# A list-scheduled attention and MLP block: products of originals in streams of their own, traced DMA constants, and new leads and places for every stage

## The chip, the cores and the metric

The kernel runs on one core of one Trainium2 chip. The metric is device time in microseconds (us) of one execution, and the median over the runs is what counts. The engines named below are TensorE (PE, matmuls and transposes), VectorE (DVE), ScalarE (ACT), GpSimd (POOL) and SyncE (SP), which here only issues DMAs.

## The reference, cut to what matters

One transformer block with cross attention, all in fp32: B = 8 batches of 256 tokens `x` with 512 features, a context of the same shape, 16 heads of 32 features, an MLP of 2048.

```python
x = layer_norm(hidden_states, ln1_w, ln1_b)
q = (x @ q_w + q_b)                     # heads of 32
k = (encoder_hidden_states @ k_w + k_b)
v = (encoder_hidden_states @ v_w + v_b)
scores = einsum('bhqd,bhkd->bhqk', q, k) * scale
scores = where(mask, scores, finfo.min)
out = einsum('bhqk,bhkd->bhqd', softmax(scores), v)
hidden = out @ cproj_w + cproj_b + residual
y = layer_norm(hidden, ln2_w, ln2_b)
y = gelu(y @ fc_w + fc_b, approximate=True) @ proj_w + proj_b
return hidden + y
```

## The kernel before

**Tiling and stages.** The batches are worked in two groups of four (`g` = 0, 1). For each group the context tiles (`ct`) and x tiles (`xt`, after a layer norm whose results are `xn`) are transposed on TensorE into `ps_c` and `ps_x` banks and copied to SBUF; then come the k, q and v projections; the attention core in 32 units per group (four heads of one batch: scores `s`, softmax `pr`, transposes of the probabilities `ps_pt`, copied to `pt`, and values `av`, scaled by reciprocals `r` into `att`); the output projection `o` with the residual `hid`; the second layer norm and its transposes `ps_y`; and the MLP products `fc` and `pr`. k, q and v are stored to DRAM (`kd`, `qd`, `vd`) and loaded again unit by unit (`ku`, `qu`, `vu`); reciprocals take the same way (`rd`, `r`).

**Seven products instead of eight.** Every large product is cut into 2x2 blocks and computed by Winograd's scheme in `quad`: seven block products P1 to P7, in the order 1, 2, 6, 7, 5, 3, 4, into three PSUM banks X, Y and W. P1 and P2 take blocks of both operands as they are (originals). P3 to P7 take a sum of blocks on at least one side: `kws`, `qws`, `vws` of the weights, `c0t` and `x0t` of the tokens, computed on VectorE or GpSimd (`plus`). P6, P5 and P3 add onto P1 in bank X. The MLP uses the scheme on two levels (`grown2`, `grown`); the sums of its weights, `fw` and `pw`, are computed during the attention core and stored to DRAM (`fcd`, `prd`); those of its inputs are `y1t`, `z1t` and `z1i` for group 1.

**What sets the order.** No loop issues instructions directly. Every operation is recorded in an `Order` with the engines that could run it and a cost on each. `times` gives each TensorE operation a due time `vt`, spread evenly over the window of its stream (`WINDOWS`, one stream per stage and group); every other operation is due ahead of its earliest user, by its own cost, for DMAs also `DMA_FIXED + 1.0 + mb / DMA_RATE`, and by its `lead`. `run` then simulates the engines, and each takes among the ready operations the one due first, under limits:

```python
if o.vt - (t - lag) > AHEAD[e]:
    continue
...
soon = bisect.bisect_left(vts.get("C", []), last + BORROW)
lent = sorted(s[0] for s in free_slots["C"])[soon:]
```

`AHEAD` is how far ahead of its due time an operation may be placed on an engine; the other two lines let `quad` borrow PSUM banks of the C kind (5, for transposes, scores and values) beside its own three, less those that a C user due within `BORROW` will want. SBUF tiles come from a pool of slots: one slot of 128x1024 holds, one after another, tiles of many names, so a row in the profile or the order shows the name that first held it (`ct` in a row may hold x tiles, `kw_222<-in_x_dram` is an x tile). The engine of each operation, and its place, are thus decided when the program is built; on the chip each engine runs its list in order.

**DMAs.** All loads and stores are issued by SP, in the order of its list, over eight semaphore lanes: a DMA is not issued before the one eight places earlier has landed. `load` and `store` record them.

**Lines the change touches.** Constants at lines 30 to 34, `times` (100), `run` with `room` (135, 177), `INPUTS` and `WINDOWS` (365 to 376), `load` (461), `mask_of` (548: a mask row is loaded into `mu` and turned into a bias `mb` on VectorE or GpSimd; the `mu` tile of batch b + 4 is that of batch b), `quad` (658) and its callers `project_turned`, `project_plain`, `keys_of`, `values_of`, and `attention_inputs` (1074), which records the loads, transposes and projections of a group.

## Time and profile before

| | |
|---|---|
| median of 3 runs | 753.72 us (751.98 to 754.6) |
| the profiled execution | 753.82 us |
| its span | 752.0 us |
| mean granted TensorE clock | 0.993 |
| DMA | 144.06 MB, mean 192 GB/s |
| ACT, largest idle group | `pr` activations, 108.0 us idle, 104.2 of it behind VectorE's `st` |

The median of the three runs is the time before. The profile is of one execution of its own, and "span" is the time from its first to its last recorded instruction. In a row of a timeline stand start, duration, engine, line, operation, tiles with shapes and, in brackets, the idle time of that engine just ahead and what ended it. In a row of a table by stretches stand, after the stretch, its length, then for PE, PEld (weight loads), DVE, ACT and POOL the busy time with the count of instructions, then the granted clock, the busy share of the DMA engines and GB/s. In a row of a group stand line, engine, operation, tiles and count, then busy time, mean ns of one, and the idle time ahead.

### The profile page before, as it was taken

What the parts mean: (1) busy time and instruction counts of PE and PEld (TensorE: products, weight loads), DVE (VectorE), ACT (ScalarE), POOL (GpSimd) and SP (SyncE); (2) the same over time, 40 slices, a digit from 0 to 9 for tenths busy, and PEclk for the clock granted to TensorE, in tenths of its full rate; (3) what the DMA queues carried; (4) which work ended last, traced back from release to release, by engine and by line L of the source; (5) the groups of instructions that cost most, each with busy time, mean ns of one, the idle gap of its engine ahead of it and who ended that gap; (6) DMA issues with size and microseconds to landing.
All of it is one profiled execution on the core that took longest, in us unless ns stands there. A gap on an engine that the chain in (4) does not pass through costs nothing.

```text
span 752.0 us, 13728 instructions
## 1 busy us (share of the span) xinstructions
PE 710.5 (94%) x4753; PEld 563.5 (75%) x4753; DVE 596.0 (79%) x1356; ACT 293.9 (39%) x829; POOL 331.4 (44%) x290
## 2 busy tenths in 40 slices
PE   6799999989999799899999999989999999899997
PEld 4345675457655577678787779989998888799997
DVE  4895788668796688788788887997688877989784
ACT  3300665448365383664556893120001034430000
POOL 2631075464640331410101388556873126859650
PEclk9999999999999899999999999999999999999999
DMA  7818889788568845355444451365767455463641
GB/s 253 293 58 311 288 274 316 222 266 283 164 223 290 279 147 188 91 159 165 136 140 145 136 194 57 118 210 173 259 214 220 147 160 169 147 229 115 223 144 57
DMA packets 119332, 144.06 MB, mean 192 GB/s; under 512 B 14136, under 2 KB 82272, under 8 KB 119264
## 3 DMA queue, kind: packets, MB, share of 16 engines
q1 hardware_dynamic: 119264, 143.19, 59.3%
q8 instruction: 38, 0.62, 0.3%
q14 instruction: 30, 0.25, 0.1%
HBM read 98.59 MB, written 44.56 MB: 190 GB/s over the span
## 4 chain that ended last, share of the span: by engine, by line
PE 77%; DVE 11%; DMA 7%; issue 3%; SPq 1%; ACT 1%; POOL 0%; DVEq 0%; POOLq 0%
PE fc_X L506 12%; PE pr_X L506 11%; PE fc_W L506 6%; PE ps_pt L831 6%; PE pr_W L506 5%; PE s L506 4%; PE o_X L506 4%; PE av L506 4%; PE q_X L506 3%; PE fc_Y L506 3%; PE v_X L506 3%; PE k_X L506 3%; PE pr_Y L506 2%; PE o_W L506 2%; PE q_W L506 2%
## 5 line engine op out<-in xcount | busy, mean ns | idle before, releaser
L808 ACT ACTIVATE pr<-pr,st 128x256 f32<-128x256 f32 x256 | 127.4, 501 | 108.0 <-DVE st L802 104.2
L802 DVE CUSTOM_DVE_ANT_0 pr<-s,mb 128x256 f32<-128x256 f32 x256 | 91.6, 419 | 10.6 <-PE s L506 10.4
L831 PEld LDWEIGHTS ps_pt<-ident,pr 128*128 128x128 f32 x512 | 59.7, 142 | 20.8 <-issue 7.2
L991 ACT ACTIVATE h<-h,cols 128x256 f32<-128x256 f32 x128 | 54.1, 499 | 51.1 <-DVE h L497 43.6
L831 PE MATMUL ps_pt<-ident,pr 128*128 128x128 f32 x512 | 71.0, 276 | 2.5 <-DVE att L497 1.5
L497 DVE TENSOR_TENSOR h<-fc_X,h 128x512 f32<-128x512 f32 x80 | 54.7, 687 | 14.2 <-PE fc_X L506 13.6
L477 ACT COPY pt<-ps_pt 128x512 f32<-128x512 f32 x87 | 48.5, 576 | 21.8 <-PE ps_pt L831 21.6
L808 ACT ACTIVATION_READ_ACCUMULATOR pr<-pr,st 128x1 f32 x256 | 48.9, 191 | 0.0
L477 ACT COPY e<-pr_X 128x256 f32<-128x256 f32 x4 | 1.5, 373 | 112.3 <-PE pr_X L506 112.3
L506 PE MATMUL av<-pt,vu 128*32 128x256 f32 x512 | 35.7, 390 | 4.1 <-DVE pt L477 3.9
L506 PE MATMUL s<-ku,qu 32*128 32x256 f32 x512 | 37.8, 400 | 0.0
L497 DVE TENSOR_TENSOR h<-fc_W,h 128x512 f32<-128x512 f32 x48 | 33.0, 688 | 4.4 <-PE fc_W L506 2.7
L506 PEld LDWEIGHTS s<-ku,qu 32*128 32x128 f32 x512 | 24.0, 184 | 14.2 <-issue 9.6
L506 PEld LDWEIGHTS av<-pt,vu 128*32 128x32 f32 x512 | 13.6, 109 | 24.0 <-issue 8.5
L497 DVE TENSOR_TENSOR po<-pr_X,po 128x256 f32<-128x256 f32 x40 | 16.7, 419 | 18.5 <-PE pr_X L506 18.5
L477 DVE COPY pt<-ps_pt 128x512 f32<-128x512 f32 x41 | 27.2, 680 | 3.1 <-PE ps_pt L831 2.8
L555 POOL TENSOR_SCALAR mb<-mu 128x256 f32<-128x256 uint8 x4 | 1.6, 404 | 52.7 <-DMA mu<-in_mask_BxS_bf_dram 52.7
L614 POOL TENSOR_TENSOR rs_y<-rs_y,neg_half 128x2 f32<-128x2 f32 x8 | 6.0, 753 | 34.5 <-DVE rs_y L611 34.5
L802 DVE DVE_READ_ACCUMULATOR2_ANT st<- 128x1 f32 x256 | 21.1, 83 | 0.0
L497 DVE TENSOR_TENSOR att<-av,r 128x256 f32<-128x256 f32 x32 | 13.5, 421 | 8.0 <-PE av L506 5.5
L497 DVE TENSOR_TENSOR h<-fc_Y,h 128x512 f32<-128x512 f32 x24 | 16.5, 686 | 2.2 <-PE fc_Y L506 1.7
L1128 POOL TENSOR_TENSOR hid<-hid,cb 128x1024 f32<-128x1024 f32 x5 | 14.1, 2822 | 8.8 <-DMA hid<-in_x_dram 5.8
(657 smaller groups left out, 1902.7 us busy)
## 6 DMA issues: line engine op xcount, KB each, us to landing
pl<-prd SPq DMA_DIRECT2D x26, 256.0 KB
fw<-in_L_xattn_fc_w_dram SPq DMA_DIRECT2D x16, 256.0 KB
ku<-kd SPq DMA_DIRECT2D x32, 128.0 KB
qu<-qd SPq DMA_DIRECT2D x32, 128.0 KB
vu<-vd SPq DMA_DIRECT2D x32, 128.0 KB
r<-rd SPq DMA_DIRECT2D x32, 128.0 KB
pw<-in_L_xattn_proj_w_dram SPq DMA_DIRECT2D x32, 128.0 KB
hid<-in_x_dram SPq DMA_DIRECT2D x8, 512.0 KB
```

The lines of the kernel that those rows point to most:

```text
L477: (nc.scalar.copy if e == "ACT" else nc.vector.tensor_copy)(to(), of_())
L497: E[e].tensor_tensor(to(), in0(), in1(), op)
L506: nc.tensor.matmul(o(), l(), r(), start=first, stop=True, skip_group_check=True)
L555: lambda e: E[e].tensor_scalar(tile_of(mb), mu.t, -1.0, FLT_MAX, ALU.add, ALU.mult), lock=True)
L614: lambda e, rs=rs: nc.gpsimd.tensor_tensor(tile_of(rs)[:, 2:4], tile_of(rs)[:, 0:2], neg_half[:, 0:2], ALU.pow), lock=True)
L802: nc.vector.tensor_tensor_reduce(at(p_, pk), at(sb[j], i), tile_of(mb), scale=-SCALE, scalar=FLT_MAX, op0=ALU.add, op1=ALU.min, accum_out= ...
L808: nc.scalar.activation(at(p_, pk), at(p_, pk), AF.Exp, bias=tile_of(st)[:, 8 + c : 9 + c], scale=-1.0, accum_out=tile_of(st)[:, 16 + c : 1 ...
L831: nc.tensor.transpose(at(ps, 2 * kc + i, 1, P), at(pr[j // 2], 2 * (j % 2) + i)[:, ts(kc, P)], ident.t)
L991: lambda e, f=f, b=b, c=c: nc.scalar.activation(at(h[f][b], c), at(h[f][b], c), AF.Gelu_apprx_tanh, bias=col(c_fcb + f * 4 + c), scale=1.0 ...
L1128: lambda e, v=v: E[e].tensor_tensor(v(), v(), cb.t[:, None, :].to_broadcast([P, 2, D]), ALU.add), lock=True)
```

## The change

It alters the planner's numbers and one part of its rules, and records some products in other streams. What is computed stays the same.

- *Streams for products of originals.* `quad` has a parameter `early`: P1, P2 and the copies behind them are recorded in that stream. In group 0 k uses `e0`, v `e1` and q `e2`. The k, v and q projections of group 0 are recorded as k0, k1, v0, q0, q1, v1 instead of k0, q0, v0, k1, q1, v1; weights are loaded in the order k, v, q instead of k, q, v.
- *DMA model.* `DMA_FIXED` 1.7 to 3.0, `DMA_RATE` 0.36 to 0.34, the SP cost of a DMA 0.45 to 0.5.
- *Leads.* A table `LEADS` adds to the lead of each load by its name (from 8.6 for `qw`, 7.7 for `pw`, 5.9 for `xt` and 3.8 for `mu` down to -1.0 for `fl` and `ku`); a mask load gets a lead of 12.0 besides.
- *Windows.* Each stream has three times instead of two, one of them for the middle of its TensorE work, and all are new numbers.
- *Limits.* `AHEAD` VectorE 40 to 66.7, ScalarE 40 to 36.8, GpSimd 40 to 25.4, SP 16 to 26.9; `BORROW` 14.0 to 25.6, where at most two C users of the light kind (`ps_` names other than `ps_pt`) count. `SWITCH` is 0.0. The cost of scores is 0.97 instead of 0.86, that of values 0.9.

```diff
-BORROW = 14.0
+BORROW = 25.6
+SWITCH = 0.0
-AHEAD = {"PE": 1000.0, "DVE": 40.0, "ACT": 40.0, "POOL": 40.0, "SP": 16.0}
+AHEAD = {"PE": 1000.0, "DVE": 66.7, "ACT": 36.8, "POOL": 25.4, "SP": 26.9}
-DMA_FIXED, DMA_RATE, DMA_LANES = 1.7, 0.36, 8
+DMA_FIXED, DMA_RATE, DMA_LANES = 3.0, 0.34, 8
...
-            t0, t1 = windows[name]
+            t0, tm, t1 = windows[name]
...
-                o.vt = t0 + (t1 - t0) * at / total
+                f = 2.0 * at / total
+                o.vt = t0 + (tm - t0) * f if f < 1.0 else tm + (t1 - tm) * (f - 1.0)
...
+        light = lambda b: b.kind == "C" and b.name.startswith("ps_") and not b.name.startswith("ps_pt")
+        vts["heavy"] = [b.vt for b in pending.get("C", []) if not light(b)]
...
-                    soon = bisect.bisect_left(vts.get("C", []), last + BORROW)
+                    heavy = bisect.bisect_left(vts["heavy"], last + BORROW)
+                    soon = heavy + min(2, bisect.bisect_left(vts.get("C", []), last + BORROW) - heavy)
...
-    [("k", 0), ("q", 0), ("v", 0), ("k", 1), ("q", 1), ("v", 1)],
+    [("k", 0), ("k", 1), ("v", 0), ("q", 0), ("q", 1), ("v", 1)],
...
-    "core0": (60, 206), "ctx1": (88, 96), "k1": (94, 130), "v1": (124, 160), "x1": (142, 152), "q1": (152, 190),
+    "core0": (68.9, 154.0, 221.0),
+    "e0": (6.3, 7.3, 8.3),
...
+LEADS = {"fl": -1.0, "res": 2.3, "mu": 3.8, "qw": 8.6, "qu": 4.4, "r": 2.3, "pw": 7.7, "ow": 1.8, "kw": 3.9, "fw": 2.8, "pl": 4.1, "vw": 2.0, "ct": 1.3, "ku": -1.0, "hid": -0.8, "xt": 5.9, "vu": 2.3}
...
-            name, [("SP", 0.45)], list(src), [(b, keys)],
-            lambda e: nc.sync.dma_start(to(), of_()), mb=mb, lead=lead,
+            name, [("SP", 0.5)], list(src), [(b, keys)],
+            lambda e: nc.sync.dma_start(to(), of_()), mb=mb, lead=lead + LEADS.get(name.rstrip("0123456789_"), 0.0),
...
-        load(f"mu{b}", mu, None, lambda: mu.t, lambda: mask[b].partition_broadcast(P), 0.03)
+        load(f"mu{b}", mu, None, lambda: mu.t, lambda: mask[b].partition_broadcast(P), 0.03, lead=12.0)
...
+        stream = T.now
+        if early:
+            T.stream(early)
         prod(1, X, True)
         out_of(X, "11", "t1", True)
         prod(2, Y, True)
         out_of(Y, "11", "c11", False)
+        T.stream(stream)
```

What the planner makes of it is seen in the built order. First the head of SP's list, the loads that begin the program; before:

```order
L464 DMA ct_0_216<-in_ctx_dram 128x512 x2
L464 DMA ct_2_219<-in_ctx_dram 128x512 x2
L464 DMA kw_222<-in_L_xattn_k_w_dram 128x2x256
L464 DMA kw_222<-in_x_dram 128x512
L464 DMA xt_1_225<-in_x_dram 128x512 x2
L464 DMA xt_3_228<-in_x_dram 128x512
L464 DMA xt_3_228<-in_ctx_dram 128x512
```

The same list of the change:

```order
L499 DMA vw_216<-in_L_xattn_v_w_dram 128x2x256
L499 DMA vw_216<-in_ctx_dram 128x512
L499 DMA ct_1_219<-in_ctx_dram 128x512 x2
L499 DMA ct_3_222<-in_ctx_dram 128x512
L499 DMA ct_3_222<-in_L_xattn_k_w_dram 128x2x256
L499 DMA kw_225<-in_L_xattn_k_w_dram 128x2x256
L499 DMA kw_225<-in_ctx_dram 128x512
```

A tile of v weights now stands ahead of the context tiles, and the x tiles that stood in places 6 to 9 come behind context and weights.

On TensorE, in the prologue behind the context transposes, before (rows 33 to 40; `k_0_X` on `c0t` and `kws` is a product of sums, `ps_x` a group of x transposes):

```order
L570 MATMUL ps_x_30_371<-ident,xn_x_00_297 128x128 x2
L570 MATMUL ps_x_30_371<-ident,xt_1_225 128x128
L570 MATMUL ps_x_30_371<-ident,xn_x_11_326 128x128
L506 MATMUL q_0_X<-x_00_347,qw_350 128x512 x2
L506 MATMUL k_0_W<-c0t_367,xt_7_344 128x512 x2
L506 MATMUL q_0_Y<-x_10_377,qw_350 128x512 x2
L506 MATMUL k_0_X<-c0t_411,kws_416 128x512 x2
L506 MATMUL k_0_X<-c0t_332,kws_358 128x512 x2
```

There of the change (rows 31 to 42, behind five products of originals):

```order
L541 MATMUL k_0_W<-c0t_324,kws_261 128x512 x2
L541 MATMUL k_1_Y<-c_10_263,kw_239 128x512 x2
L541 MATMUL k_0_X<-c0t_328,vw_216 128x512 x2
L541 MATMUL v_1_X<-vw_216,c_00_246 128x256 x4
L541 MATMUL k_0_X<-c0t_318,kws_261 128x512 x2
L541 MATMUL v_1_Y<-kw_239,c_10_263 128x256 x4
L541 MATMUL k_0_X<-c_11_305,ct_3_222 128x512 x2
L541 MATMUL k_0_W<-c0t_342,ct_7_231 128x512 x2
L541 MATMUL k_1_X<-c0t_328,vw_216 128x512 x2
L541 MATMUL k_1_W<-c0t_324,kws_261 128x512 x2
L541 MATMUL k_1_X<-c0t_318,kws_261 128x512 x2
L605 MATMUL ps_x_00_478<-ident,qws_431 128x128
```

Before, all four x groups of the first tokens and the first q products stand among the k products; now 16 products of k and v stand ahead of the first x transposes, of which six groups follow one another from there.

On SP at the loads of group 1's x tiles (the `in_x_dram` rows; `prd` rows store sums of proj weights, `mu_129` is a mask load), before:

```order
L464 DMA ku_1465<-kd_0_12_131 128x256
L464 DMA qu_1472<-qd_0_12_135 128x256
L470 DMA prd_116<-pw0s_1447 128x4x256
L464 DMA mu_129<-in_mask_BxS_bf_dram 128x256
L470 DMA vd_1_11_150<-kws_358 128x512
L464 DMA ct_7_246<-in_x_dram 128x512
L464 DMA kws_416<-in_x_dram 128x512
L464 DMA xt_7_344<-in_x_dram 128x512
```

The same place of the change:

```order
L499 DMA vu_1517<-vd_0_22_141 128x2x128
L499 DMA kw_239<-in_x_dram 128x512
L499 DMA vw_216<-in_x_dram 128x512
L499 DMA kws_261<-in_x_dram 128x512
L499 DMA xt_3_1557<-in_x_dram 128x512
L505 DMA vd_1_11_150<-k_0_21_385 128x512
L499 DMA xt_3_1557<-in_x_dram 128x512
```

The x loads now stand ahead of every `prd` store. The two mask loads of group 1 that stood at rows 218 (`mu_170`, four rows ahead of the residual `hid_0`) and 227 of SP's list stand at rows 194 and 196 of the new one:

```order
L499 DMA vu_2078<-vd_1_11_150 128x2x128
L499 DMA mu_170<-in_mask_BxS_bf_dram 128x256
L499 DMA ku_2094<-kd_1_22_137 128x256
L499 DMA mu_172<-in_mask_BxS_bf_dram 128x256
L499 DMA vu_2105<-vd_1_21_152 128x2x128
```

The conversions of both to `mb` are on GpSimd in the new order, where one of them was on VectorE.

On TensorE around the transposes of the second layer norm of group 0 (`ps_y`), before:

```order
L831 MATMUL ps_pt_2_3018<-ident,pr_1_2744 128x128 x4
L831 MATMUL ps_pt_3_3025<-ident,pr_1_2744 128x128 x4
L506 MATMUL o_1_X<-kws_416,att_11_1280 128x256 x4
L506 MATMUL av_3044<-pt_0_2998,vu_2791 32x256 x2
L506 MATMUL av_3044<-pt_1_3033,vu_2791 32x256 x2
...
L506 MATMUL o_1_W<-vws_466,a0t_2812 128x256 x4
L570 MATMUL ps_y_01_3095<-ident,xn_y_20_3016 128x128 x2
```

And in the change (rows 536 to 540 of 1085, behind which stand seven more rows of scores, the four of one `av` and then the last four rows here):

```order
L541 MATMUL o_1_W<-qws_431,a0t_2770 128x256 x4
L870 MATMUL ps_pt_1_3112<-ident,pr_0_2845 128x128 x4
L870 MATMUL ps_pt_2_3119<-ident,pr_1_2852 128x128 x4
L870 MATMUL ps_pt_3_3128<-ident,pr_1_2852 128x128 x4
L541 MATMUL s_0_3142<-ku_2926,qu_2903 128x256
...
L870 MATMUL ps_pt_1_3190<-ident,pr_0_2971 128x128 x4
L870 MATMUL ps_pt_2_3206<-ident,pr_1_2978 128x128 x4
L870 MATMUL ps_pt_3_3213<-ident,pr_1_2978 128x128 x4
L605 MATMUL ps_y_00_3220<-ident,vw_216 128x128
```

Where `ps_y` stood right behind the last output product `o_1_W`, seven groups of probability transposes, eight rows of scores and one block of values stand between. On VectorE the list has 9 more sums of 128x1024, 13 more of 128x256 and 6 more copies of 128x512 than before; the sums among them were GpSimd's.

## The prediction before the run

> **What bounds the kernel now.** I read the page first: span, busy shares, and the chain of work that ended last.
>
> ```profile
> span 752.0 us, 13728 instructions
> PE 710.5 (94%) x4753; PEld 563.5 (75%) x4753; DVE 596.0 (79%) x1356; ACT 293.9 (39%) x829; POOL 331.4 (44%) x290
> PE 77%; DVE 11%; DMA 7%; issue 3%; SPq 1%; ACT 1%; POOL 0%; DVEq 0%; POOLq 0%
> ```
>
> TensorE is busy for 710.5 of 752.0 us, and the change leaves every matmul in place: it alters order and engine choice, not the 4753 matmul records. So TensorE's work stays, and what can be won or lost is the 752.0 − 710.5 = 41.5 us in which it idles, plus time in which its clock is halved. The execution itself took 753.82 us, 1.82 us more than its span, and lies 0.1 us over the median shown (753.72), so the sum is made against 753.8.
>
> Next I read TensorE's own rows in order of time, looking only for those with idle time ahead of them (in brackets: how long, and what ended it). The prologue first:
>
> ```profile
> 3.54 1.04 PE L570 MATMUL ps_c<-ident,ct 128*128 128x128 f32 x2 [3.54 <-DMA ct<-in_ctx_dram]
> 5.40 0.48 PE L570 MATMUL ps_c<-ident,ct 128*128 128x128 f32 x1 [0.82 <-DMA ct<-in_ctx_dram]
> 6.74 3.04 PE L570 MATMUL ps_c<-ident,ct 128*128 128x128 f32 x13 [0.86 <-DMA ct<-in_ctx_dram]
> 12.38 0.33 PE L570 MATMUL ps_c<-ident,ct 128*128 128x128 f32 x1 [0.28 <-DMA ct<-in_ctx_dram]
> 13.04 0.33 PE L570 MATMUL ps_c<-ident,ct 128*128 128x128 f32 x1 [0.33 <-DMA ct<-in_ctx_dram]
> 14.71 0.23 PE L541 MATMUL ps_cols<-ident,rows 40*128 40x40 f32 x1 [0.47 <-ACT c L477]
> 22.00 1.96 PE L506 MATMUL q_X<-x,qw 128*128 128x512 f32 x4 [3.00 <-DMA qw<-in_L_xattn_q_w_dram]
> 31.37 1.98 PE L506 MATMUL k_X<-c0t,kws 128*128 128x512 f32 x4 [2.26 <-DVE kws L484]
> 39.86 1.95 PE L506 MATMUL q_W<-x0t,vw 128*128 128x512 f32 x4 [1.12 <-DVE x0t L497]
> ```
>
> The first three (5.22 us) are the start: the context tiles arrive one after another. The other six, 0.28 + 0.33 + 0.47 + 3.00 + 2.26 + 1.12 = 7.46 us, are waits for inputs that were asked for in an unlucky order: q products before the q weights had landed, seventh-products before VectorE had their sums and drains.
>
> In the middle of the kernel three waits stand out, and each is explained by the VectorE row ahead of it:
>
> ```profile
> 145.58 2.01 DVE L497 TENSOR_TENSOR pw0s<-pw,pw 128x1024 f32<-128x1024 f32 x1 [1.98 <-DMA pw<-in_L_xattn_proj_w_dram]
> 148.74 1.23 DVE L497 TENSOR_TENSOR pw0s<-pw,pw0s 128x1024 f32<-128x1024 f32 x1 [1.16 <-POOL pw0s L495]
> 150.36 0.66 PE L831 MATMUL ps_pt<-ident,pr 128*128 128x128 f32 x4 [1.50 <-DVE att L497]
> 157.49 0.69 DVE L605 BATCH_NORM_STATS2 st_x<-ct 128x6 f32<-128x512 f32 x1 [4.24 <-DMA ct<-in_x_dram]
> 158.88 1.98 PE L506 MATMUL k_X<-c,kws 128*128 128x512 f32 x4 [3.55 <-DVE xt L484]
> 243.32 0.47 SPq L464 DMA_DIRECT2D mu<-in_mask_BxS_bf_dram  x1
> 248.61 0.29 DVE L555 TENSOR_SCALAR mb<-mu 128x256 f32<-128x256 uint8 x1 [6.11 <-DMA mu<-in_mask_BxS_bf_dram]
> 250.16 1.91 PE L506 MATMUL av<-pt,vu 128*32 128x256 f32 x10 [3.92 <-DVE pt L477]
> ```
>
> VectorE takes its instructions in order. At 157.49 it had stood 4.24 us before the first statistics of group 1's x because that tile had not landed; the drain behind it, which TensorE needed, came late by the same. At 248.61 it had stood 6.11 us for a mask load issued only at 243.32, and copies of transposed probabilities waited behind. TensorE's 1.50 + 3.55 + 3.92 = 8.97 us are thus **late loads, seen through VectorE**.
>
> The last large one is the second layer norm of group 0, and two tables by stretch show what the long waits did to the clock (the number after the engines):
>
> ```profile
> 302.84 0.33 PE L570 MATMUL ps_y<-ident,xt 128*128 128x128 f32 x1 [2.83 <-DVE xt L627]
> 304.43 0.81 PE L570 MATMUL ps_y<-ident,xn_y 128*128 128x128 f32 x2 [0.87 <-ACT xn_y L625]
> 250.00:255.00 5.00, 4.84 (x19) 3.15 (x20) 3.17 (x8) 0.00 (x0) 2.49 (x2) 0.50 0.90 278
> 255.00:260.00 5.00, 5.00 (x43) 3.22 (x42) 4.43 (x18) 2.00 (x9) 3.94 (x2) 0.88 0.78 271
> 300.00:310.00 10.00, 6.30 (x43) 5.14 (x43) 6.71 (x17) 3.18 (x4) 4.83 (x7) 0.83 0.41 128
> ```
>
> After the mask wait the granted clock was 0.50 for 5 us and 0.88 for the next 5: 2.5 + 0.6 = 3.1 us of matmul time lost beyond the wait itself. After the layer norm's 2.83 + 0.87 = 3.70 us it was 0.83 over 10 us: 1.7 us more. What remains of the 41.5, some 16 us (41.5 − 5.22 − 7.46 − 8.97 − 3.70), is scattered in small waits and the end.
>
> **The change part by part.** *Start.* The changed queue puts a v-weight tile ahead of the context tiles, so the four that the first transposes need come one place later. Issues that wait for a landing eight places earlier give the pace:
>
> ```profile
> 8.30 0.33 SPq L464 DMA_DIRECT2D rows<-in_L_xattn_ln_w_dram  x1
> 8.97 0.25 SPq L464 DMA_DIRECT2D rows<-in_L_xattn_ln_b_dram  x1
> ```
>
> One 256 KB tile takes 8.97 − 8.30 = 0.67 us there; TensorE's rows at 5.40 and 6.74 put it at 1.34 us. I take the middle: **+1.0** (0.7 to 1.3).
>
> *Prologue.* Of the 7.46 us, the q-weight wait goes because the q products now stand behind 16 k and v products. Each of those is a row of somewhat under 2 us like the k_X row above, so they cover some 28 us, and the x tiles, q weights and layer norm have that long to arrive; the queue asks for them right behind the bias rows. The waits for kws and x0t go for the same reason: between the first k product and the first that needs sums (k_0_W) there are now three more products of originals and 16 transposes, about 7 us, while VectorE has three weight sums, one copy and two token sums ahead of it, at 0.7 us for 512 columns (half of the 1.23 above, and a little) and 1.2 for 1024, about 5 us. What is late next is the drain of the x transposes, of which six groups now stand together with five banks to write to: no row of before has it; between nothing and the 2.26 + 1.12 of today's VectorE waits, I take 1.0, nearer the x rows of before, which waited little. **−6.5** (−7.5 to −4.1).
>
> *Late loads.* The two mask loads that begin group 1 stand 24 and 31 places earlier on the queue, and both conversions are on GpSimd, so VectorE's queue holds neither; x of group 1 is asked for before any store of proj-weight sums instead of behind the first, so it no longer waits for that sum. The 3.55 and 3.92 us and the 3.1 us of clock go. The proj sums still stand on VectorE behind a GpSimd sum, so of the 1.50 I keep 0.5. 8.97 + 3.1 − 0.5: **−11.6** (−12.1 to −4.6, where one wait and clock loss like the mask's, 3.92 + 3.1 = 7.0, comes back).
>
> Whether a wait costs clock too is seen in the stretch of the x wait, which shows none:
>
> ```profile
> 150.00:200.00 50.00, 45.39 (x298) 33.42 (x299) 38.59 (x128) 29.92 (x86) 26.74 (x35) 1.00 0.83 263
> ```
>
> [...]
>
> *Layer norm of y.* Before, the transposes stand right behind the last output product. Now seven groups of transposes, one block of scores and one of values stand between.
>
> ```profile
> 243.33 2.35 PE L831 MATMUL ps_pt<-ident,pr 128*128 128x128 f32 x20
> 145.80 1.15 PE L506 MATMUL s<-ku,qu 32*128 32x256 f32 x16
> 296.80 1.07 PE L506 MATMUL av<-pt,vu 128*32 128x256 f32 x16
> ```
>
> Five groups of four take 2.35, so seven 3.3; with 1.15 and 1.07 it is 5.5 us of cover for a chain that now shows 3.70 us of waits. VectorE has other rows among that chain (score maxima), so I do not count it whole: of 3.70 + 1.7 = 5.4 I take **−3.5** (−5.4 to 0).
>
> *Work moved to VectorE.* Counted over the built order, VectorE has 9 more sums of 128x1024, 13 more of 128x256 and 6 more drains of 128x512, GpSimd the fewer; most of it late: of the proj operands of group 1 (z1t, z1i) ten sums move.
>
> ```profile
> L497 DVE TENSOR_TENSOR z1i<-z1t,z1i 128x1024 f32<-128x1024 f32 x7 | 12.0, 1720 | 0.0
> L497 DVE TENSOR_TENSOR z1t<-h,h 128x1024 f32<-128x1024 f32 x3 | 3.7, 1217 | 0.0
> 640.00:660.00 20.00, 18.08 (x92) 14.80 (x91) 18.90 (x23) 9.56 (x23) 16.49 (x12) 1.00 0.52 171
> 660.00:680.00 20.00, 19.36 (x171) 18.98 (x170) 17.14 (x18) 4.85 (x13) 12.57 (x7) 1.00 0.62 206
> 680.00:700.00 20.00, 18.82 (x167) 18.55 (x166) 19.21 (x22) 0.00 (x0) 18.85 (x11) 1.00 0.31 99
> ```
>
> Ten at 1.22 are 12.2 us on an engine with 60 − 18.90 − 17.14 − 19.21 = 4.8 us free in those three slices: 7.4 too many if all fell there and nothing else changed. Yet the same sums last 1.72 beside a busy GpSimd and 1.22 in the other row; if the seven z1i fell to 1.22, 3.5 of it came back, and the order begins the sums earlier. Bounds 0 and 7.4, I take **+2.0**, nearer to nothing, because both rows speak for relief.
>
> [...]
>
> Elsewhere the small waits are moved about, not known to shrink: 0, with half of 16 us either way.
>
> **Sum:** 753.8 + 1.0 − 6.5 − 11.6 − 3.5 + 2.0 = **735.2**, so 735.
>
> **The rivals.** *VectorE becomes the bound late.* For it: the 7.4 us above, and fc's second half also gains sums. Against it: the relief just named. It costs 7.4 instead of 2.0, and a long wait with its clock loss of 1.7 on top: 742.
>
> *Held queue, slower.* Loads may now be placed up to 26.9 us ahead of their due time instead of 16. A load whose buffer is not yet free holds the whole SP queue, and the reciprocals and score inputs of core1 behind it come late. Price as the mask's: 7.0 per hold. Two leave the kernel faster (749); from the third on it is slower: 735.2 + 21 = 756. Against it: the largest waits on late loads today are the ones that the earlier loads remove.
>
> *Waits only move.* The new order fits the planner's numbers and not the chip: each removed wait turns up elsewhere, since VectorE is busier. 751.5 to 756.
>
> **How the numbers follow.** The forecast 0.74; late VectorE 0.10; waits that only move 0.08; held queue 0.08. The first two are faster, so faster by over 0.3% (2.3 us, about what a measurement of this kernel can tell from no change) has 0.84, within it 0.08, slower 0.08. The low end takes every gain whole, no new VectorE cost and 6.5 of the small waits' 8: 753.8 + 0.7 − 7.5 − 12.1 − 5.4 − 6.5 = 723. The high end takes the poor bounds of all terms but the layer norm, of which it keeps 2: 753.8 + 1.3 − 4.1 − 4.6 − 2 + 7.4 = 751.8, so 752; it holds the late-VectorE rival.
>
> **What would show it.** Right: no TensorE wait of over 1 us between 12 and 40 us; no VectorE wait on mask or x loads after that; full clock from 20 us to the end, or one dip at most; y's transposes waiting under 2 us; VectorE's 1024-wide z1 sums nearer 1.2 than 1.7. Wrong: TensorE rows after 600 us waiting on VectorE for over 8 us in all, or rows in core1 that wait for r, qu or vu.

## The result and the profile after

The changed kernel takes 720.92 us in the median of 4 runs (719.78 to 721.54), the kernel before 754.16 beside it (751.98 to 755.11): ratio 0.9561, 95% interval 0.9537 to 0.9586. The forecast was 735 with a range from 723 to 752; the direction was right, and the time lies 2.1 us under the low end. The profiled execution took 720.62 us.

From the page of the changed kernel, its span, the busy shares and the chain that ended last:

```profile
span 718.6 us, 13665 instructions
PE 699.8 (97%) x4753; PEld 563.0 (78%) x4753; DVE 592.1 (82%) x1382; ACT 294.5 (41%) x829; POOL 281.3 (39%) x261
PE 90%; DVE 6%; DMA 2%; issue 1%; SPq 0%; POOL 0%; DVEq 0%; POOLq 0%
```

TensorE's share of the chain went from 77 to 90%, VectorE's from 11 to 6 and DMA's from 7 to 2. The first line to stop at is TensorE's busy time: the same 4753 matmuls, and 10.7 us less (710.5 to 699.8). Idle time fell by 22.7 (41.5 to 18.8); the two make the 33.4 us of span.

So busy time held losses too. A better measure goes by starts: for each two matmul records that follow one another, the distance of their starts less the one that such pairs show in both traces when nothing holds them (in the median 0.109 us for a 128-wide transpose, 0.112 for a proj matmul of 128, 0.216 for 256 columns, 0.429 for 512, and 0.094 more where scores or values begin or end). This sum, with the time to the first matmul, is TensorE's loss. By stretches of the span, in us:

| stretch | before | after | change | in the forecast |
|---|---|---|---|---|
| 0-50 (prologue, start) | 17.4 | 9.3 | -8.1 | -5.5 |
| 50-140 | 3.1 | 2.4 | -0.7 | 0 |
| 140-230 (x of group 1) | 9.8 | 5.1 | -4.7 | late loads, |
| 230-290 (masks; o) | 9.4 | 2.4 | -7.0 | together -11.6 |
| 290-330 (second layer norm) | 6.4 | 1.1 | -5.3 | -3.5 |
| 330-600 | 12.0 | 4.0 | -8.0 | 0 |
| 600 to the end | 6.7 | 7.9 | +1.2 | +2.0 |
| all | 64.8 | 32.2 | -32.6 | -18.6 |

The prologue after the change, TensorE's rows in order of time:

```profile
10.46 1.95 PE L541 MATMUL v_X<-vw,c 128*128 128x256 f32 x8
...
19.43 1.98 PE L541 MATMUL k_X<-c,ct 128*128 128x512 f32 x4
21.25 1.88 PE L541 MATMUL k_W<-c0t,kws 128*128 128x512 f32 x4
22.97 1.88 PE L541 MATMUL k_Y<-c,kw 128*128 128x512 f32 x4
...
41.79 0.62 PE L605 MATMUL ps_x<-ident,xn_x 128*128 128x128 f32 x2
...
44.73 1.45 PE L541 MATMUL q_X<-x,xt 128*128 128x512 f32 x3
```

None has a bracket: from 10.46 to the first q product nothing waits long enough to show. The first product of sums (k_W) begins 1.82 us behind its neighbour, 0.1 above the pace of such products (four at 0.429). In the kernel before, the first product began at 9.57:

```profile
9.57 1.89 PE L506 MATMUL k_X<-c,kw 128*128 128x512 f32 x3
```

What VectorE waited for on DMAs, from the table of waits of VectorE (total, times, longest), before:

```profile
DVE mb L555 <- DMA mu<-in_mask_BxS_bf_dram: 7.4, 2, 6.1
DVE st_x L605 <- DMA ct<-in_x_dram: 4.2, 1, 4.2
DVE st_x L605 <- DMA kws<-in_x_dram: 3.0, 2, 1.9
DVE pw0s L497 <- DMA pw<-in_L_xattn_proj_w_dram: 2.0, 1, 2.0
```

and after:

```profile
DVE kws L532 <- DMA ct<-in_L_xattn_k_w_dram: 2.7, 1, 2.7
DVE att L532 <- DMA r<-rd: 2.6, 1, 2.6
```

Mask, x and proj-weight loads are gone from it. The second layer norm's transposes now stand behind probability transposes and find their input there:

```profile
281.85 2.72 PE L870 MATMUL ps_pt<-ident,pr 128*128 128x128 f32 x16
284.60 0.33 PE L605 MATMUL ps_y<-ident,vw 128*128 128x128 f32 x1
284.77 0.27 PE L605 MATMUL ps_y<-ident,q 128*128 128x128 f32 x1
```

One long wait is new, late in the last product; here the rows of TensorE and of VectorE ahead of it:

```profile
644.21 1.95 PE L541 MATMUL pr_X<-e,z1i 128*128 128x128 f32 x16
...
651.43 3.04 PE L541 MATMUL pr_X<-pl,z1t 128*128 128x128 f32 x16 [3.48 <-DVE po L532]
654.26 4.42 PE L541 MATMUL pr_W<-pl,z1i 128*128 128x128 f32 x32
...
645.15 2.28 DVE L532 TENSOR_TENSOR z1i<-h,h 128x1024 f32<-128x1024 f32 x1
647.36 1.48 DVE L532 TENSOR_TENSOR po<-po,res 128x256 f32<-128x256 f32 x1
648.76 2.28 DVE L532 TENSOR_TENSOR z1i<-h,z1i 128x1024 f32<-128x1024 f32 x1
650.96 0.41 DVE L532 TENSOR_TENSOR po<-pr_X,po 128x256 f32<-128x256 f32 x1
```

The drain at 650.96 is that of the product begun at 644.21 and could have run at 646.2, when it had ended; it stood behind a residual sum and a sum of 2.28 us. The matmuls behind the wait run slower (3.04 instead of 1.95 for sixteen); the granted clock was 0.73 from 650 to 655 us and 0.93 from there to 660.

### The profile page after: what moved, and what is told of

It reads as the page before. It is cut to its first block, busy times and chain, and to the rows that moved or that the text cites. A ratio compares the mean times of both kernels' runs of the same rounds, so it can differ in the third digit from the quotient of the medians.

```text
span 718.6 us, 13665 instructions
## 1 busy us (share of the span) xinstructions
PE 699.8 (97%) x4753; PEld 563.0 (78%) x4753; DVE 592.1 (82%) x1382; ACT 294.5 (41%) x829; POOL 281.3 (39%) x261
## 4 chain that ended last, share of the span: by engine, by line
PE 90%; DVE 6%; DMA 2%; issue 1%; SPq 0%; POOL 0%; DVEq 0%; POOLq 0%
PE fc_X L541 13%; PE pr_X L541 13%; PE ps_pt L870 7%; PE fc_W L541 7%; PE pr_W L541 7%; PE s L541 5%; PE av L541 4%; PE k_X L541 4%; PE o_X L541 4%; PE q_X L541 4%; PE v_X L541 3%; PE fc_Y L541 3%; PE pr_Y L541 3%; PE o_W L541 2%; PE q_W L541 2%; PE v_W L541 2%
## 5 line engine op out<-in xcount | busy, mean ns | idle before, releaser
L870 PEld LDWEIGHTS ps_pt<-ident,pr 128*128 128x128 f32 x512 | 59.4, 141 | 18.5 <-issue 5.6
L532 POOL TENSOR_TENSOR h<-h,fl 128x512 f32<-128x512 f32 x8 | 11.1, 1396 | 55.5 <-DVE fl L532 54.9
L530 POOL TENSOR_TENSOR z0t<-h,h 128x512 f32<-128x512 f32 x12 | 15.0, 1272 | 13.3 <-PE fc_X L541 11.6
L530 POOL TENSOR_TENSOR z0i<-z0t,z0t 128x512 f32<-128x512 f32 x10 | 16.4, 1660 | 6.3 <-DVE y1t L532 3.3
```

What stands on the lines that cost most here:

```text
L530: nc.gpsimd.tensor_tensor(to()[:, ts(k, 512)], in0()[:, ts(k, 512)], in1()[:, ts(k, 512)], op)
L532: E[e].tensor_tensor(to(), in0(), in1(), op)
L870: nc.tensor.transpose(at(ps, 2 * kc + i, 1, P), at(pr[j // 2], 2 * (j % 2) + i)[:, ts(kc, P)], ident.t)
```

## The experiments

The kernels are of two kinds. In the *pinned* ones the built list is kept, and after it is made single operations are moved in it: `move("a", "b")` puts operation a directly ahead of b. In the others numbers or rules of the planner are set, and it builds a new list. Ratios are to the kernel before, timed beside each; 0.3% are 2.3 us.

| run | median us | ratio (95%) | loss |
|---|---|---|---|
| changed kernel | 720.92 | 0.9561 (0.9537-0.9586) | 32.2 |
| e1 masks early (before, pinned) | 754.77 | 0.9999 (0.9977-1.002) | 67.1 |
| e2 drains ahead (before, pinned) | 753.03 | 0.9993 (0.9967-1.0018) | 64.1 |
| e5 masks and cb early (before, pinned) | 751.08 | 0.9953 (0.9931-0.9976) | 60.9 |
| e3 late drains (change, pinned) | 717.77 | 0.9509 (0.9475-0.9542) | 25.2 |
| e4 no early streams | 727.34 | 0.9653 (0.962-0.9686) | 39.5 |
| e6 loads part only (on before) | 740.67 | 0.9821 (0.9791-0.985) | 53.6 |
| e7 loads part undone | 737.74 | 0.977 (0.9727-0.9814) | 53.0 |
| e8 limits undone | 721.13 | 0.9569 (0.9535-0.9603) | 37.9 |
| e9 windows undone | 738.39 | 0.9785 (0.9743-0.9827) | 47.6 |
| e10, e16, e18 three draws on the change | 712.81, 721.83, 719.25 | 0.9438, 0.9581, 0.9545 | 25.3, 32.0, 31.1 |
| e15 a draw on before | 748.46 | 0.9921 (0.9894-0.9948) | 60.2 |
| e11 three sums to VectorE | 718.88 | 0.9506 (0.9458-0.9554) | 32.7 |
| e12 more drains, start | 713.98 | 0.9451 (0.9419-0.9484) | 26.3 |
| e13 no overlap | 716.81 | 0.9522 (0.9475-0.957) | 29.6 |
| e14 overlap only (on before) | 754.32 | 1.0017 (0.998-1.0055) | 65.2 |
| e17 first draw, a drain ahead | 710.96 | 0.9438 (0.9404-0.9472) | 21.1 |

The loss is TensorE's loss by starts, as above. It is that of the one profiled execution, which may lie some us from the median (e3's took 713.20 with a median of 717.77, e8's 725.66 with a median of 721.13).

**Late loads one at a time (e1, e5, e2).**

e1, on the list of the kernel before, moves the loads of two masks:

```diff
+    move("mu4", "ku033")
+    move("mu6", "qu033")
```

> The kernel before with its built order kept and one thing moved: the two mask loads that begin group 1 stand on SP's list between the same loads as in the changed kernel. Theory 1 (late loads, priced as in the prediction): VectorE's 6.1 us wait on the mask goes, TensorE's 3.9 us wait behind it and the half clock after it (3.1) too, so 7.0 us less than before, 747, and a granted clock of 1.00 between 250 and 260 us. Rival (waits only move): something else on VectorE or on the queue holds TensorE at the same place; less than 2 us gained, 752 to 754.

e1 gained nothing, though the mask wait is gone. VectorE's row that waits next, and TensorE's behind it, in e1:

```profile
253.20 1.68 DVE L1128 TENSOR_TENSOR hid<-hid,cb 128x1024 f32<-128x1024 f32 x1 [4.25 <-DMA cb<-in_L_xattn_cproj_b_dram]
...
258.96 1.11 PE L831 MATMUL ps_pt<-ident,pr 128*128 128x128 f32 x4 [5.01 <-DVE st L802]
```

In the kernel before, the cb load was hidden behind the late mask: it came to 0.58 us. With the mask early it is the next to hold VectorE. So e5 has a third move:

```diff
+    move("cb", "prd1_1_True")
```

> The kernel before with its built order kept; the two mask loads stand earlier as in the run that moved them alone, and the load of the output projection's bias (cb), on which VectorE stood 4.25 us in that run, stands 25 places earlier too. Theory 2 (a chain of late loads: behind each one that VectorE waits for stands the next): with both early, VectorE's next late input is the sums of ow weights, some 1.5 us; TensorE loses 3 to 5 us less between 230 and 290 us than before (9.4 there), 749 to 751. Rival (the DMA queue, not its order, is what is short there: each load moved up delays the others by as much): still over 8 us lost between 230 and 290, total within 2 us of before.

With all three early the loss from 230 to 290 falls from 9.4 to 7.0, less than the 3 to 5 us of theory 2, and the total by 0.47%, some 3.5 us. What VectorE waits for next in e5 is no load but a sum on GpSimd, longer than the 1.5 us expected:

```profile
251.06 0.69 DVE L497 TENSOR_TENSOR v<-kw,kws 128x512 f32<-128x512 f32 x1 [3.67 <-POOL kw L497]
```

The late mask did hold VectorE, as the forecast says, but other late inputs stand behind it, so that taking it away alone is worth nothing: the rival "waits only move" holds for e1, and a chain, of loads first and then of a sum, for e5.

e2, on the list of the kernel before, leaves the x load where it is and moves two drains on VectorE:

```diff
+    move("k1_1_t3", "stats_x1_00")
+    move("k1_1_c22", "stats_x1_00")
```

> The kernel before with its built order kept and one thing moved: two drains of k sums (k_X into a tile first held by xt, and k_W added to it) stand on VectorE ahead of the first layer-norm statistics of group 1's x, not behind them. The x load stays where it was. Theory 1 (VectorE's order makes TensorE wait for a load that TensorE doesn't need): TensorE's 3.55 us go, 750.2. Rival (the x tile itself is what is late: its statistics, layer norm and x transposes come no earlier, and TensorE waits for them or for the next drain instead): within 1 us of before.

TensorE's 3.55 us wait for the drain is gone from e2's profile, but another grew (for att, 1.5 to 2.2), the clock fell at other places (0.63 from 20 to 25 us, 0.69 from 25 to 30, 0.83 from 150 to 160 and 0.66 from 300 to 310, where the kernel before has 1.00, 1.00, 1.00 and 0.83), and the total can't be told from before. An earlier x load was not tried in the old list.

**The parts of the change (e6, e7, e4, e8, e9).**

e6 puts the loads part into the kernel before, e7 takes the same out of the changed one; beside these lines it is the mask lead of 12.0, the SP costs of 0.5 and `LEADS` in `load`:

```diff
-AHEAD = {"PE": 1000.0, "DVE": 40.0, "ACT": 40.0, "POOL": 40.0, "SP": 16.0}
+AHEAD = {"PE": 1000.0, "DVE": 40.0, "ACT": 40.0, "POOL": 40.0, "SP": 26.9}
-DMA_FIXED, DMA_RATE, DMA_LANES = 1.7, 0.36, 8
+DMA_FIXED, DMA_RATE, DMA_LANES = 3.0, 0.34, 8
```

> The kernel before with the part on loads alone: DMA constants, SP costs, SP's limit of 26.9, LEADS and the mask lead of 12 of the change; old windows, streams, other limits. Theory 3 (each part carries its own term): the loads part is worth the late-loads term and some of the prologue, 740 to 746. Rival (the numbers were found together and work together): without the new windows the earlier loads hold the queue or find no free tile, and the total is within 4 us of before or slower, 750 to 760.

> The changed kernel with the part on loads undone: DMA constants, SP costs, SP's limit, LEADS and the mask lead as before; new windows, streams and other limits. Theory 3: about 12 us come back, 730 to 735, as VectorE waits on mask, x or cb loads. Rival (the windows alone put the loads where they are early enough): under 4 us slower than the changed kernel. If parts work only together, more than 15 us slower.

e4 takes the early streams out of the changed kernel, for q and v as here for k:

```diff
-                keys_of("k", g, i, W["k"], Cop, c_kb, kd, "e0" if g == 0 else None)
+                keys_of("k", g, i, W["k"], Cop, c_kb, kd)
```

> The changed kernel without the streams e0, e1, e2: P1 and P2 of group 0 are recorded in the streams of k, v and q again; windows, leads and all else stay. Theory 1 (the v and k products of originals cover VectorE's first sums): TensorE waits 2 to 4 us in the prologue, 723 to 725, and most of the prologue's gain is lost. Rival (the new windows alone put the x transposes behind enough k products): no TensorE wait over 1 us between 12 and 45 us, within 2 us of the changed kernel in the prologue, and what differs in the total comes from later.

e8 takes the limits out of it, with the rule on banks:

```diff
-BORROW = 25.6
+BORROW = 14.0
-AHEAD = {"PE": 1000.0, "DVE": 66.7, "ACT": 36.8, "POOL": 25.4, "SP": 26.9}
+AHEAD = {"PE": 1000.0, "DVE": 40.0, "ACT": 40.0, "POOL": 40.0, "SP": 26.9}
```

> The changed kernel with the limits undone: AHEAD of VectorE, ScalarE and GpSimd 40, BORROW 14 and the old rule on banks; all else new. Theory 4 (more bank borrowing and work placed further ahead is what took the small waits out of 330 to 600 us, 12.0 us lost before, 4.1 after): 5 to 8 us come back there, 726 to 729. Rival (the places of the stages did it): 330 to 600 us loses under 6 us, total within 3 us of the changed kernel.

e9 has the `WINDOWS`, `INPUTS` and order of weights of before, no early streams, and this line behind the old table:

```diff
+WINDOWS = {n: (a, (a + b) / 2, b) for n, (a, b) in WINDOWS.items()}
```

> The changed kernel with the windows of before (the middle time set halfway), its order of projections and weights, and no early streams; the loads part, the limits and the bank rule of the change stay. Theory 5 (the parts add up: loads about 14, early streams 6.4, limits nothing, the rest the new windows): 740, as the loads part alone on the kernel before (740.7), within 4 us. Rival (the limits matter where the windows are old): more than 4 us away from 740.

The loads part alone takes the kernel before to 740.67, 13.9 us less than before beside it, a size that theory 3 allows. Taken back from the changed kernel it costs 16.8, some 3 more than theory 3 allowed and past the 15 that would speak for parts that work only together; the 13.9 of e6 alone speaks against that.

By place the loads part is not the late-loads term. In e6 the two masks of group 1 hold VectorE no longer, but one of group 0, which this list converts on VectorE, does; TensorE waits behind it, with a granted clock of 0.50 in the 5 us that follow:

```profile
139.05 0.29 DVE L557 TENSOR_SCALAR mb<-mu 128x256 f32<-128x256 uint8 x1 [7.17 <-DMA mu<-in_mask_BxS_bf_dram]
...
140.68 2.82 PE L833 MATMUL ps_pt<-ident,pr 128*128 128x128 f32 x12 [4.00 <-DVE st L804]
...
140.00:145.00 5.00, 4.32 (x15) 3.29 (x15) 5.00 (x20) 4.68 (x16) 0.00 (x0) 0.50 0.76 234
```

Between 50 and 290 us e6 wins only some 5 us of loss, where the whole change wins 12.4. In e7, with the old loads and the new windows, VectorE waits for no mask, and of the 20.8 us that it loses more than the changed kernel 11.1 lie between 330 and 600 (15.1 instead of 4.0). Either part by itself thus takes VectorE's wait for group 1's masks away, and more than half of what the loads part is worth lies elsewhere.

Without the early streams the time is 6.4 us longer, more than theory 1 expected: without them q's first product of sums waits again, and the first context tile comes later, as two k-weight tiles stand ahead of it. From e4's table of TensorE's waits:

```profile
PE ps_c L605 <- DMA ct<-in_ctx_dram: 7.2, 3, 6.0
PE q_W L541 <- DVE x0t L532: 2.5, 1, 2.5
```

Most of it is the prologue's: its loss is 14.2 there, 9.3 with them. Without the new limits the ratio is the same (0.9569 against 0.9561). What e9 has over e4, windows and the order of projections and weights, is 738.39 - 727.34 = 11 us. Loads 14 to 17, windows 11, early streams 6 and limits 0 add up to 31 to 34, against 33 measured, and e9 came out near where the loads part alone had (740.67). Each of these figures is the difference of two single lists, though, and lists that differ by a mere draw, below, lie up to 9 us apart.

By stretches the windows carry the second layer norm. Its stretch loses 6.8 with loads alone and old windows (e6) and 3.5 in e9, where a further wait of 2.75 us for the same transposes, ended at 291.76, falls into the stretch ahead by the edge at 290; with the new windows it is between 0.8 and 1.9 in every list.

**The stretch from 330 to 600 (e8, e13, e14).**

e13, on the changed kernel, lets fc1 begin where pr0 ends:

```diff
-    "pr0": (422.3, 480.5, 534.1),
-    "fc1": (488.4, 556.6, 620.7),
-    "pr1": (623.6, 650.2, 752.3),
+    "pr0": (422.3, 478.7, 535.0),
+    "fc1": (535.0, 585.0, 635.0),
+    "pr1": (636.0, 662.0, 752.3),
```

> The changed kernel with three windows changed: fc1 begins where pr0 ends (535 instead of 488.4) and pr1 behind it, so that their products no longer alternate (3 changes between the two on TensorE's list, as in the kernel before, instead of 41 in the changed kernel). Theory 8 (pr0 alone keeps VectorE too busy for TensorE, mixed with fc1 it doesn't): 330 to 600 us loses 7 to 12 us instead of 4.1, total 724 to 729. Rival (other places did it: o1, y1, the end of fc0): under 5.5 us lost there, total 719 to 723.

e14, on the kernel before, lets the two overlap:

```diff
-    "pr0": (390, 496), "fc1": (496, 582), "pr1": (582, 670),
+    "pr0": (390, 485), "fc1": (446, 558), "pr1": (561, 670),
```

> The kernel before with three windows changed and nothing else: fc1 from 446 to 558, pr0 to 485, pr1 from 561, which has 41 changes between pr0 and fc1 instead of 3. Theory 8: 330 to 600 us loses 4 to 8 us less than the 12.0 of before, total 746 to 750. Rival: the loss stays over 10, total within 2 us of before.

Theory 8 falls twice. Without the overlap this stretch loses 4.4, not 7 to 12, and the kernel is no slower than the change (0.9522 against 0.9561, with intervals that overlap). With the overlap put into the kernel before, it still loses 10.4, and what it gains there is lost again after 600 (6.7 to 8.7). The limits may take part (8.0 lost there in e8, but that execution took 4.5 us more than the median of its runs, which is that of the change), and so do the loads: 7.7 in e6 with loads alone, 15.1 in e7 with new windows and old loads. No single part is shown to hold these 8 us; which of them removes which of the small waits stays open.

**How much is the draw of a list (e10, e16, e18, e15).**

These lines behind the windows, with seed 1 in e10, 2 in e16 and 3 in e18 on the changed kernel, and 1 in e15 on the kernel before:

```diff
+_r = random.Random(1)
+WINDOWS = {n: tuple(sorted(t + _r.uniform(-1.0, 1.0) for t in w)) for n, w in WINDOWS.items()}
```

> The changed kernel with each time of its windows moved by a random amount of up to 1 us either way (one draw). Theory 6 (what the new windows gain is where the stages stand, to some us): within 4 us of the changed kernel, 717 to 725. Rival (the windows were fitted to this one list, and any other list of the same planner has a wait of some us somewhere): 727 to 740, with one or more TensorE waits of over 2 us that the changed kernel doesn't have.

> The changed kernel with a second random draw of up to 1 us on each time of its windows. Theory 9: 712 to 728, on either side of the changed kernel. Rival (the windows are good to a us and the first draw was an exception): over 728.

> The changed kernel with a third random draw of up to 1 us on each time of its windows. Theory 9 (lists of one set of windows spread over some 10 us): 710 to 728. Rival: over 728.

> The kernel before with each time of its windows moved by a random amount of up to 1 us either way (one draw). Theory 9 (any list of this planner is a draw with a spread of some 5 to 8 us, and the change moved the middle of the spread): 746 to 762. Rival (the list of before was an unlucky one and the change partly a lucky draw): under 742.

The first draw left the band of theory 6 on the side that nobody had named. Moving every window time by up to 1 us gives 712.8, 721.8 and 719.3 where the change has 720.9, and 748.5 where the kernel before has 753.7. A list is a draw with a spread of some 9 us over these four, and the two families lie about 30 apart (the old one with only two lists): the gain is no lucky draw, and the numbers of the change are not the best of their own neighbourhood. It also limits the runs above that build a new list. What e4, e8 and e13 differ by from the changed kernel, 6.4, 0.2 and 4.1 us, is within that spread, so that the time alone does not show what their edits are worth; e4 has its prologue rows besides.

**The late wait and the load on VectorE (e3, e11, e12, e17).**

e3, on the list of the changed kernel, moves three drains on VectorE:

```diff
+    move("pr16_t3", "out1_0021")
+    move("pr16_c22", "out1_0021")
+    move("pr12_t2", "z1i2_4")
```

> The changed kernel with its built order kept and one thing moved: where TensorE waits 3.48 us at 651 us for the drain of a pr_X product, three drains (pr_X, pr_W, pr_X) stand on VectorE ahead of the last z1i sum and the residual sum that they stood behind. Theory 1 (the late bound on VectorE is the order of its list): TensorE's 3.48 us and the lower clock behind it (some 1.8) go, 715.6 against 720.9. Rival (VectorE has no time left there, so the sum that now comes later is waited for by the next products): within 1.5 us of the changed kernel.

In e3 the drain runs as its product ends, and the wait is gone; rows of VectorE and TensorE at that place:

```profile
645.19 0.41 DVE L532 TENSOR_TENSOR po<-pr_X,po 128x256 f32<-128x256 f32 x1
...
645.65 2.05 PE L541 MATMUL pr_X<-pl,z1t 128*128 128x128 f32 x16
```

The loss after 600 us falls from 7.9 to 2.8, the median by 3.2 us against the 5.3 expected. e11 is e3 with three GpSimd sums on VectorE, at their places:

```diff
+    for o in order:
+        if o.name in ("z1i6_4", "z1i5_1", "z1i5_2"):
+            o.eng = "DVE"
```

> The changed kernel's list with the three drains moved as in the run before that did so, and three GpSimd sums of 128x1024 (z1i, at 639 to 650 us in the changed kernel) on VectorE at their places. Theory 7 (a GpSimd sum takes from VectorE nearly what the sum costs there: VectorE's sums last 2.26 beside it and 1.22 alone): VectorE's busy time from 635 to 665 us grows by under 1.5 us, its z1i sums there last 1.2 to 1.3, and the total is within 2 us of the run with the drains alone (717.8). Rival (VectorE's count of sums decides): VectorE grows by 3.7 us, TensorE waits that much more for drains there, 720 or more.

Stretches of 31 us around the same products, first e3, then e11, 6 us later there (busy time of PE, PEld, DVE, ACT, POOL):

```profile
629.00:660.00 31.00, 30.88 (x276) 30.63 (x275) 29.58 (x36) 2.08 (x5) 14.69 (x9) 1.00 0.24 69
```

```profile
635.00:666.00 31.00, 30.19 (x267) 29.76 (x266) 28.77 (x38) 2.08 (x5) 5.00 (x3) 1.00 0.21 60
```

GpSimd's busy time falls by 9.7 us, and VectorE's does not rise: 29.58 to 28.77. One group of those sums, in e3 and then in e11 (busy time, mean ns):

```profile
L532 DVE TENSOR_TENSOR z1i<-h,z1i 128x1024 f32<-128x1024 f32 x4 | 6.5, 1613 | 0.0
```

```profile
L532 DVE TENSOR_TENSOR z1i<-h,z1i 128x1024 f32<-128x1024 f32 x4 | 4.9, 1215 | 0.0
```

The total (718.88) is that of e3 within the interval. Theory 7 holds for these three sums: on GpSimd they took no load off VectorE.

e12 is e3 with three more drains and the first v-weight tile moved:

```diff
+    move("fc114_t3", "z1t1_1")
+    move("fc004_t3", "z0i1_1")
+    move("fc111_c22", "y1t2")
+    move("vw00", "kw00")
```

> The changed kernel's list with the three drains moved as before, three more (an fc_X drain ahead of a z1t sum at 618 us, an fc_X drain ahead of a z0i sum at 410, an fc_W drain ahead of a y1t sum at 522), and the v-weight tile that heads SP's list put behind the first four context tiles. Theory 1: 0.9 + 0.4 + 0.6 of waits go and the start is some 0.7 us earlier, 2 to 3 us less than with the three drains alone, 715 to 716. Rival (sums that come later are waited for): within 1 us of 717.8.

It takes 713.98, 3.8 less than e3 where 2 to 3 were expected. Drains and start are not told apart in it; its first product begins at 8.93, earlier than in the changed kernel (10.46) and in that before. e17, on the list of the first draw (e10), moves two sums behind a drain:

```diff
+    move("fc107_21", "fc117_c22")
+    move("z1i1_2", "fc117_c22")
```

> The list of the first random draw (712.8) with one thing moved: where TensorE waits 1.52 us at 607 us for a drain of an fc_X product, that drain stands on VectorE ahead of an h sum and a z1i sum instead of behind them. Theory 1 (the order of VectorE's list): 1 to 1.5 us less, 711 to 712. Rival (the sums are waited for then): 712.5 or more.

It takes 710.96, 1.9 us less than e10 by the medians, but the ratios to the kernel beside them are the same (0.9438), so that the edit's gain is not shown. It is the fastest median seen, 5.6% under the kernel before.

## Why the prediction was right in direction and wrong in size

- *Start, +1.0.* Right: first product at 10.46 instead of 9.57, +0.9; e12 takes it back.
- *Prologue, -6.5.* The cover was right, all six waits went, and it was worth 9.0 (8.1 and the start's 0.9). The term was mis-sized twice. Six waits of 7.46 us idle cost 8.5 by starts (0.44, 0.55, 0.63, 3.16, 2.43, 1.28), since the record of the matmul ahead of a wait lasts longer than the pace (0.27 us instead of 0.109 ahead of the q weights' wait) and covers the first part of it. And the 1.0 kept for the drains of six x groups did not come: the one stop there, at 41.79, is 0.2.
- *Late loads, -11.6.* The size agrees (140 to 290: 19.2 lost before, 7.5 after, -11.7), in part by luck. The waits did go, but the price put on each did not hold: e1 shows that the two masks, priced at 7.0, give nothing alone, e5 that a third load is needed for even half, and e6 that the loads part alone brings some 5 of the 12.4 us between 50 and 290. The x load was misread as well: it did not wait for the store of proj sums. SP's rows of before show the store issued in 0.38 us and the x load right after two more, and the statistics that needed it began at 157.49, 6.4 us after its issue:

```profile
149.13 0.38 SPq L470 DMA_DIRECT2D prd<-pw0s  x1
...
151.13 0.75 SPq L464 DMA_DIRECT2D ct<-in_x_dram  x1
```

- *Layer norm of y, -3.5.* The cover held whole: -5.3, the far bound of the term.
- *VectorE, +2.0.* +1.2 by the stretch, but for another reason. One wait of 3.48 us, with the clock of 0.73 behind it, is over half of what is lost there, and e3 removes it by order alone. Three of the sums, moved to VectorE in e11, cost it nothing, so the late-VectorE rival named the right place and, as far as that goes, the wrong cause.
- *Elsewhere, 0: the step that failed.* "Elsewhere the small waits are moved about, not known to shrink: 0, with half of 16 us either way." They shrank by 8.7 (0.7 from 50 to 140 and 8.0 from 330 to 600), more than half of the 14.0 us by which the loss fell further than the forecast's sum; the prologue's 2.5 and the layer norm's 1.8 come next. Behind it stands the first number of the argument, that 41.5 us of idle time and some time at a lower clock (3.1 + 1.7) are all that can be won. By starts it was 64.8: at least 18.5 us of short stops, slow matmuls and first parts of long waits lay inside TensorE's busy time. Half of the unnamed rest, 21.8 by starts (3.1, 12.0 and 6.7), would have put the low end 4.4 lower than the 6.5 did, at some 719. What removed the 8.0 stays open, as said above.

Of the signs of being right all came, the last one narrowly: no long wait in the prologue, no VectorE wait for masks or group 1's x, one dip of the clock while TensorE has work (0.73 from 650 to 655, 0.93 to 660), no wait of y's transposes, and VectorE's 1024-wide z1 sums at a mean of 1.42 us (1.67 before). Of the rivals, held queue did not come: no row in TensorE's table of waits names r, qu or vu. VectorE's one wait for r, 2.60 us at 159.78, is ahead of core1. What would have shown the steps wrong did not appear either: TensorE waits for VectorE after 600 us come to 4.9 us (3.48, 0.90 and 0.52), under the 8 set.

## What to carry to other kernels

Measure what can be won on an engine by the starts of its instructions, not by its idle time: back-to-back pace is read from the pairs of each kind that nothing holds, and the rest is loss, whether the profile calls it busy or idle (here 64.8 us by starts against 41.5 idle). A wait removed alone can show the next late input behind it (e1), and putting right what makes loads late, here the planner's idea of a load's time, gained 13.9 us and still left VectorE 7.17 us behind one mask (e6). Where a planner builds the list, time a few neighbours of its numbers before a difference of 1% is put down to a reason, and look for drains that stand behind long sums: moving them gained in e3, and with the start in e12, though not in e2, and in e17 no gain is shown.

## What the runs showed of the hardware

**A wait of the same length cost clock in one execution and none in another.** The wait for the q weights was 3.00 us in the kernel before, with full clock after it, and 2.94 in e2, whose list is the same up to there. The stretches behind it, of the kernel before and then of e2 (the granted clock is the number after the engines):

```profile
20.00:25.00 5.00, 3.00 (x7) 1.44 (x8) 5.00 (x13) 0.97 (x2) 2.37 (x2) 1.00 1.08 354
25.00:30.00 5.00, 4.11 (x10) 1.52 (x8) 4.69 (x6) 0.00 (x0) 5.00 (x5) 1.00 1.05 327
```

```profile
22.04 3.75 PE L506 MATMUL q_X<-x,qw 128*128 128x512 f32 x4 [2.94 <-DMA qw<-in_L_xattn_q_w_dram]
...
20.00:25.00 5.00, 2.96 (x4) 1.44 (x5) 5.00 (x13) 0.38 (x1) 2.40 (x2) 0.63 1.06 341
25.00:30.00 5.00, 5.00 (x9) 1.99 (x9) 2.25 (x3) 0.69 (x1) 5.00 (x5) 0.69 1.05 332
```

Four matmuls take 3.75 us instead of 1.96, the next four 3.15 instead of 1.88, and it lasts some 6 us. In these two executions the length of the wait alone did not tell its price, and neither did it within the one of the kernel before: behind the 3.55 us at 158.88 the clock stayed at 1.00, behind the 3.92 us at 250.16 it was 0.50 for 5 us. Over the 23 runs beside e1 to e4 the kernel before had a mean clock from 0.982 to 0.993 and 751.44 to 757.97 us, the changed kernel in four 0.995 to 0.998 and 719.78 to 721.54; that lists with few long waits are steadier is not shown, since e16 took 717.23 to 724.55 in four runs with a clock from 0.997 to 1.0.

**A short instruction ended when the GpSimd sum beside it did.** VectorE's scalar step of the layer norm, two columns wide, in the changed kernel, once beside GpSimd sums and once beside none:

```profile
160.02 1.40 POOL L532 TENSOR_TENSOR pw0i<-pw 128x256 f32<-128x256 f32 x2
161.38 0.72 POOL L532 TENSOR_TENSOR pw0i<-pw0i,pw 128x256 f32<-128x256 f32 x1
...
160.12 2.00 DVE L652 SCALAR_TENSOR_TENSOR rs_x<-mv_x,rs_x 128x2 f32<-128x2 f32 x1
...
162.65 0.14 DVE L652 SCALAR_TENSOR_TENSOR rs_x<-mv_x,rs_x 128x2 f32<-128x2 f32 x1
```

2.00 us instead of 0.14, and it ends (162.12) as the third of the sums does (162.10). Three more of these steps in the changed kernel, at 459.32, 473.42 and 477.24, take 1.22 or 1.23 us and end within 0.03 us of a GpSimd sum; beside none they take 0.13 to 0.16. Together with e11, where 9.7 us less of GpSimd's work left VectorE busy for 28.77 us against 29.58, it says that in these places GpSimd was no second place for fp32 sums: what it took was taken from VectorE, and from its shortest steps too.
